# Reflecting q and k per head, one product for two, and raw gathers that take turns, in a graph attention kernel

## The chip, the cores and the metric

The kernel runs on one core of one Trainium2 chip. A core has five engines that run their own instruction streams: TensorE (PE, matrix products), VectorE (DVE), ScalarE (ACT), GpSimd (POOL) and SyncE (SP, which only issues transfers). They meet through semaphores. Matrix products land in a small memory called PSUM and everything else is worked on in SBUF; tensors in device memory are reached by DMA. The metric is the device time of the whole program in microseconds (us), as the median of several runs. Each run is compared with runs of the kernel before.

## The reference

One graph attention layer with a norm ahead of it. There are N = 12500 nodes with F = 128 features and E = 212500 edges, sorted by their destination `dst`. Each edge has 128 features of its own (`edge_h`) and a weight (`distance`).

```python
h = jnp.maximum(_layernorm(x, axis=-1), 0.0)          # node_h
q = (node_h @ Wq.T + bq).reshape(N, 8, 16)
k = (edge_h @ Wk.T + bk).reshape(-1, 8, 16)
v = (node_h @ Wv.T + bv).reshape(N, 8, 16)
qs, qd = q[src], q[dst]
in_m   = jnp.sum(qs * k,  axis=-1)
out_m  = jnp.sum(qd * k,  axis=-1)
diag_m = jnp.sum(qs * qd, axis=-1)
score = (softmax(in_m * SCALE) + softmax(out_m * SCALE)
         + softmax(diag_m * SCALE)) * distance ** lam   # softmax over the edges of each dst
h = segment_sum(score[..., None] * v[dst], dst)
return x + leaky_relu(h @ Wo.T + bo, 0.1)
```

The three sums are inner products within a head of 16 numbers. An orthogonal map of each head that is applied to q and to k leaves all three unchanged.

## The kernel before, in words

The edges are worked off in blocks of 512, each as 4 tiles of 128 edges (JN = 4). There are 415 full blocks, counted by `g`, and 20 edges left over ("few"). Five blocks (S = 5) make a tile `t`, one from each of five strands of the sorted edges; there are 83 tiles, and `s` is the strand of a block.

The order of the work is written out by hand: the helper `pin` chains every instruction that it is given to the one pinned before on the same engine, so that each engine runs in the order of the program text.

*Stage one* (the loop over `g` from -2 to 24) makes `q` of all nodes and stores it in a table in device memory, `q_table`. Each of its 25 turns takes 4 tiles of 128 nodes: statistics for the norm on DVE (L1064), the norm and rectifier on ACT (L932), a transpose on PE with a copy on ACT (L939, L941), q by PE from `wq` (L947), the bias added by DVE (L950), and the store by SP (L951). The list `side` puts other work between. The q rows of sources are later fetched by an indirect DMA of POOL (L706), 4 to a block, in the function `gather`. The first 24 blocks (RAW) are gathered from the raw `x`, before `q_table` exists, and normalized and projected later, in the loop; that is 96 gathers. 60 of these are issued at turn -2 and 36 at turn 9. Gathers from `q_table` begin after every turn has stored its part.

*The main loop* runs over the 415 blocks. For block `g` it issues, in this order: the gather of block g + 26 (LOOK = 26), the load of edge features, `turn(g + 2)` (PE transposes of the edge features, L1247, ACT copy L1249), `spread_q(g + 1)` (PE spreads q of the destinations over the edges by a one-hot matrix, L1264, ACT copy L1267), `project(g + 1)` (k by PE: a bias product L1254 over 512 columns, then four products with `wk`, L1256), `logits(g)` and `one_hots(g + 3)` (ACT, L697 and L698). `logits` is four DVE operations: source q by spread q (L1275), source q by k (L1276), spread q by k (L1277), and a reduction over the 16 numbers of a head of all three (L1278). After this come, depending on `s`, the segment softmax and the sums over destinations of an earlier tile (`turn_max`, `powers`, `show_ends` with L1423 to L1427, `to_rows` with L1437), and the node tiles that become due.

The table `behind` ties the four gathers of a block to PE's progress: the first (j = 0) of block g + 1 + 26 waits for PE's `turn`, the second for `spread_q`, the third for `project` and the fourth for the last PE instruction of the iteration. PSUM holds one buffer of `eT_ps` and two each of `k_ps` and `qd_ps`.

On PE the middle of the loop reads so, for one block of it (names: `eT_ps` the transposed edge features, `qd_ps` the spread q, `k_ps` the projected k, `oh` the one-hot matrix, `win` the q rows of the destinations):

```order
L1247 MATMUL eT_ps<-ident,ea 128x128 x4
L1264 LDWEIGHTS oh
L1264 MATMUL qd_ps<-win,oh 128x128
L1264 LDWEIGHTS oh
L1264 MATMUL qd_ps<-win,oh 128x128
L1264 LDWEIGHTS oh
L1264 MATMUL qd_ps<-win,oh 128x128
L1264 LDWEIGHTS oh
L1264 MATMUL qd_ps<-win,oh 128x128
L1254 LDWEIGHTS ones_88
L1254 MATMUL k_ps<-b_94,ones_88 128x512
L1256 MATMUL k_ps<-wk,eT 128x128 x4
```

The spread of q stands ahead of the projection, and the bias product, 512 columns wide, opens the projection.

Of the kernel before, what the change touches and what calls it, by code (L numbers as in the profile page):

```python
# [7 lines left out]
F32 = mybir.dt.float32  # L8
# [3 lines left out]
ALU = mybir.AluOpType  # L12
# [460 lines left out]
def ordered_path(ctx: ExitStack, tc: tile.TileContext, flag, x, src, dst, edge_attr, edge_weight,  # L473
# [102 lines left out]

    eps = consts.tile([P, 1], F32, name="eps")
# [17 lines left out]
    bv3, bk3, bo3 = [b3[:, i, None, :].to_broadcast([3, JN, F]) for i in range(3)]  # L595
    bq_all = consts.tile([P, F], F32, name="bq_all")
# [105 lines left out]
    def gather(g):  # L702
        if g < end:
            qq = qqs[g] = firsts[g] if g < FIRST else gath.tile([P, JN, F], F32, name="qq")
            for j in range(JN):
                rows = pin(nc.gpsimd.indirect_dma_start(  # L706
                    out=qq[:, j, :], out_offset=None, in_=x if g < RAW else q_table,
                    in_offset=bass.IndirectOffsetOnAxis(
                        ap=sources[g // S][:, g % S, j:j + 1], axis=0)))
# [63 lines left out]
    with tc.tile_pool(name="prep", bufs=1) as prep, \  # L773
# [4 lines left out]
        lam_sb = prep.tile([RW, 1], F32, name="lam_sb")  # L778
        w_in = prep.tile([P, 4, F], F32, name="w_in")
# [24 lines left out]
        pin(nc.sync.dma_start(bq_all, bq[None, :].to_broadcast([P, F])))  # L804
# [99 lines left out]

        def turn_w(i, to):
# [143 lines left out]
        turn_w(0, wq)  # L1049
# [189 lines left out]
    with tc.tile_pool(name="work", bufs=2) as work, \  # L1239
            tc.tile_pool(name="scan", bufs=2) as scan, \  # L1240
            tc.tile_pool(name="ps", bufs=1, space=PSUM) as ps:
        ks, eTs, qds, q_ps, lTs = {}, {}, {}, {}, {}
# [9 lines left out]
        def project(g):  # L1252
            k_ps = ks[g] = ps.tile([P, JN, F], F32, name="k_ps", bufs=2)
            pin(nc.tensor.matmul(k_ps, ones3, bk3, start=True, stop=False))  # L1254
            for j in range(JN):
                pin(nc.tensor.matmul(k_ps[:, j, :], eTs[g][:, j, :], wk, start=False,  # L1256
                                     stop=(j == JN - 1)))
            del eTs[g]

        def spread_q(g):  # L1260
            s, d = g % S, st[g // S]
            qd_ps = q_ps[g] = ps.tile([P, JN, F], F32, name="qd_ps", bufs=2)
            for j in range(JN):
                pin(nc.tensor.matmul(qd_ps[:, j, :], ohs[g][:, j * P:(j + 1) * P],  # L1264
                                     d["win"][:, s, :], start=(j == 0), stop=(j == JN - 1)))
            qds[g] = work.tile([P, JN, F], F32, name="qd")
            pin(nc.scalar.copy(qds[g], qd_ps))  # L1267
            del ohs[g]

        def logits(g):  # L1270
            s, t = g % S, g // S
            if s == 0:
                lTs[t] = scan.tile([P, JN, S, H3], F32, name="lT", bufs=4)
            prod = work.tile([P, JN, 3, F], F32, name="prod", bufs=1)
            pin(nc.vector.tensor_mul(prod[:, :, 1, :], qqs[g], q_ps[g]))  # L1275
            pin(nc.vector.tensor_mul(prod[:, :, 0, :], qqs[g], ks[g]))  # L1276
            pin(nc.vector.tensor_mul(prod[:, :, 2, :], qds[g], ks[g]))  # L1277
            pin(nc.vector.tensor_reduce(lTs[t][:, :, s, :],  # L1278
                                        prod.rearrange("p j i (h d) -> p j (i h) d", d=DIM), AX.X,
                                        ALU.add))  # L1280
            del ks[g], qds[g], q_ps[g], qqs[g]
# [397 lines left out]
        turn(0)  # L1679
        spread_q(0)  # L1680
        project(0)
        turn(1)
        raw_rectify(SOON)
        for g in range(end):
# [115 lines left out]
        names = ("eT_ps", "k_ps", "qd_ps", "qd_ps", "k_ps")  # L1800
        for r in range(len(rest) + 2):
            if r < len(rest):
# [5 lines left out]
                of.project_o(ps.tile([P, JN, F], F32, name=names[r], bufs=1 if r == 0 else 2))  # L1808
# [48 lines left out]
```

## Time and profile before

| what | value |
|---|---|
| median of 3 runs | 2730.74 us (2729.23 to 2732.47) |
| profiled execution | 2727.95 us |
| its span, first to last instruction | 2726.2 us |
| granted clock of PE, mean | 0.745 |
| busy share PE / DVE / ACT / POOL | 71% / 76% / 52% / 58% |
| stage one ends, first gather from `q_table` | 206.72 us |
| last gather | 2542.90 us |

In the profile each line of a group gives the source line, engine, operation, what it writes and reads, the count, then busy time in us and the mean of one in ns, then the idle time of the engine just ahead of it and what ended that. "remote" as the end of a wait is an event of a semaphore for which the profile shows no instruction; "issue" is time in which the engine waited for nothing that is shown. A timeline row gives start and length in us first.

### The profile page before, as it was taken

What the parts mean: (1) busy time and instruction counts of PE and PEld (TensorE: products, weight loads), DVE (VectorE), ACT (ScalarE), POOL (GpSimd) and SP (SyncE); (2) the same over time, 40 slices, a digit from 0 to 9 for tenths busy, and PEclk for the clock granted to TensorE, in tenths of its full rate; (3) what the DMA queues carried; (4) which work ended last, traced back from release to release, by engine and by line L of the source; (5) the groups of instructions that cost most, each with busy time, mean ns of one, the idle gap of its engine ahead of it and who ended that gap; (6) DMA issues with size and microseconds to landing.
All of it is one profiled execution on the core that took longest, in us unless ns stands there. A gap on an engine that the chain in (4) does not pass through costs nothing.

```text
span 2726.2 us, 37924 instructions
## 1 busy us (share of the span) xinstructions
PE 1941.1 (71%) x10956; PEld 1524.3 (56%) x10956; DVE 2071.3 (76%) x2887; ACT 1409.7 (52%) x2662; POOL 1585.3 (58%) x1683
## 2 busy tenths in 40 slices
PE   2366776777767777677777777777777776777885
PEld 1245655555555555555555655656556565555664
DVE  2265887777778778778877878877878787787995
ACT  1355864445555555555545555554545555555673
POOL 7516566666666666666666666666666666666200
PEclk9876887776777777777667767766767677776786
DMA  6256444544454454544445444444444544454431
GB/s 177 76 165 175 133 123 126 141 140 127 132 146 132 134 147 140 138 138 125 140 121 137 131 128 132 131 130 123 128 141 112 140 135 121 128 139 129 125 85 52
DMA packets 378950, 355.75 MB, mean 130 GB/s; under 512 B 192898, under 2 KB 298637, under 8 KB 378527
## 3 DMA queue, kind: packets, MB, share of 16 engines
q1 hardware_dynamic: 310109, 238.12, 30.6%
q0 software_dynamic: 53184, 108.92, 15.1%
q10 hardware_dynamic: 15440, 6.20, 0.9%
q8 instruction: 90, 1.47, 0.2%
q14 instruction: 127, 1.04, 0.1%
HBM read 320.83 MB, written 32.17 MB: 129 GB/s over the span
## 4 chain that ended last, share of the span: by engine, by line
PE 44%; DVE 16%; ACT 13%; another core or an unknown queue 12%; issue 11%; DMA 1%; DVEq 1%; POOL 1%; SPq 0%; ACTq 0%; POOLq 0%
PE k_ps L1256 12%; PE w_ps L1437 7%; PE eT_ps L1247 7%; DVE lT L1278 4%; PE qd_ps L1264 4%; PE k_ps L1254 3%; PE node_ps L1186 2%; DVE prod L1276 2%; ACT qd L1267 2%; ACT relb L697 2%; DVE prod L1275 2%; DVE prod L1277 2%; ACT oh L698 2%; PE m_ps L1381 2%
## 5 line engine op out<-in xcount | busy, mean ns | idle before, releaser
L706 POOL DMA_INDIRECT qq<-q_table,sources x1564 | 1479.2, 946 | 912.7 <-issue 336.7
L1278 DVE TENSOR_REDUCE lT<-prod 128x96 f32<-128x1536 f32 x415 | 727.4, 1753 | 14.3
L1256 PE MATMUL k_ps<-wk,eT 128*128 128x128 f32 x3320 | 621.5, 343 | 18.8 <-issue 17.1
L1256 PEld LDWEIGHTS k_ps<-wk,eT 128*128 128x128 f32 x3320 | 524.3, 240 | 171.6 <-issue 170.6
L1247 PE MATMUL eT_ps<-ident,ea 128*128 128x128 f32 x1660 | 346.5, 345 | 206.6 <-issue 129.7
L1276 DVE TENSOR_TENSOR prod<-qq,k_ps 128x512 f32<-128x512 f32 x412 | 280.7, 681 | 203.5 <-remote 166.3
L1247 PEld LDWEIGHTS eT_ps<-ident,ea 128*128 128x128 f32 x1660 | 247.9, 178 | 286.2 <-issue 173.1
L1249 ACT COPY eT<-eT_ps 128x512 f32<-128x512 f32 x415 | 240.7, 580 | 322.8 <-remote 122.6
L1267 ACT COPY qd<-qd_ps 128x512 f32<-128x512 f32 x415 | 244.8, 590 | 313.1 <-PE qd_ps L1264 88.5
L1437 PE MATMUL w_ps<-back,sel 128*126 128x144 f32 (+1 forms) x1296 | 232.1, 356 | 169.0 <-ACT sel L1427 134.4
L1275 DVE TENSOR_TENSOR prod<-qq,qd_ps 128x512 f32<-128x512 f32 x412 | 279.9, 679 | 89.2 <-issue 47.9
L1437 PEld LDWEIGHTS w_ps<-back,sel 128*126 128x126 f32 (+1 forms) x1296 | 218.2, 247 | 183.4 <-ACT sel L1427 144.2
L697 ACT ACTIVATE relb<-relb,before 126x512 bf16<-126x512 bf16 x415 | 303.1, 730 | 0.0
L1277 DVE TENSOR_TENSOR prod<-qd,k_ps 128x512 f32<-128x512 f32 x415 | 281.8, 679 | 0.0
L698 ACT ACTIVATE oh<-relb 126x512 bf16<-126x512 bf16 x415 | 261.3, 630 | 13.2
L1264 PE MATMUL qd_ps<-win,oh 126*128 126x128 bf16 x1660 | 205.6, 258 | 26.6 <-issue 13.7
L1254 PE MATMUL k_ps<-b,ones 3*128 3x512 bf16 x415 | 191.4, 461 | 23.0 <-DVE prod L1277 10.9
L1264 PEld LDWEIGHTS <-oh 126*128 126x128 bf16 x1660 | 164.2, 120 | 48.0 <-issue 34.1
L1381 PE MATMUL m_ps<-ident,m 120*128 120x120 f32 x332 | 76.1, 364 | 107.6 <-issue 59.0
L1426 ACT ACTIVATE sel<-d_ps 128x420 f32<-128x420 f32 x168 | 78.5, 514 | 139.0 <-remote 127.7
L1391 ACT ACTIVATE back<-back 128x480 f32<-128x480 f32 x83 | 50.0, 602 | 142.6 <-DVE back L1390 63.2
L1381 PEld LDWEIGHTS m_ps<-ident,m 120*128 120x128 f32 x332 | 53.1, 215 | 124.5 <-issue 82.6
(234 smaller groups left out, 1934.9 us busy)
## 6 DMA issues: line engine op xcount, KB each, us to landing
ea<-in_edge_attr_dram SPq DMA_DIRECT2D x415, 256.0 KB
relb<-rel_d SPq DMA_DIRECT2D x83, 630.0 KB
qq<-q_table,sources POOLq DMA_INDIRECT x1564
win<-q_table SPq DMA_DIRECT2D x415, 31.5 KB
far<-far_d SPq DMA_DIRECT2D x84, 120.2 KB
q_table<-q SPq DMA_DIRECT2D x24, 384.0 KB
sums<-rows SPq DMA_DIRECT2D x411, 7.9 KB
q_table<-xq SPq DMA_DIRECT2D x24, 256.0 KB
```

Source lines behind the costliest of these rows:

```text
L697: pin(nc.scalar.activation(d, d, AF.Abs, bias=before[:K3]))
L698: pin(nc.scalar.activation(oh, d, AF.Relu, bias=1.0, scale=-1.0))
L706: rows = pin(nc.gpsimd.indirect_dma_start(out=qq[:, j, :], out_offset=None, in_=x if g < RAW else q_table, in_offset=bass.IndirectOffsetOn ...
L1247: pin(nc.tensor.transpose(eT_ps[:, j, :], eas[g][:, j * F:(j + 1) * F], ident))
L1256: pin(nc.tensor.matmul(k_ps[:, j, :], eTs[g][:, j, :], wk, start=False, stop=(j == JN - 1)))
L1264: pin(nc.tensor.matmul(qd_ps[:, j, :], ohs[g][:, j * P:(j + 1) * P], d["win"][:, s, :], start=(j == 0), stop=(j == JN - 1)))
L1267: pin(nc.scalar.copy(qds[g], qd_ps))
L1275: pin(nc.vector.tensor_mul(prod[:, :, 1, :], qqs[g], q_ps[g]))
L1276: pin(nc.vector.tensor_mul(prod[:, :, 0, :], qqs[g], ks[g]))
L1277: pin(nc.vector.tensor_mul(prod[:, :, 2, :], qds[g], ks[g]))
L1278: pin(nc.vector.tensor_reduce(lTs[t][:, :, s, :], prod.rearrange("p j i (h d) -> p j (i h) d", d=DIM), AX.X, ALU.add))
L1437: pin(nc.tensor.matmul(w_ps[:(hi - lo) * W, lo:hi].rearrange("p s c -> p (s c)"), d["sel"][:n, j, lo:hi, :].rearrange("p s w -> p (s w)"), ...
```

## The change

Three parts.

First, q and k are reflected per head. From the bias of k a reflection (Householder) is made for each head that maps this bias to a multiple of the first axis. It is applied to `wq` and `wk` when they are turned (a product with the reflected identity, `axes`, instead of a transpose) and to q's bias. The bias of k then has one number other than zero per head, and its product covers 4 x 8 = 32 columns; it comes after the four products with `wk`. The reflection is computed in `bring_to_size` before stage one's loop and `reflect` at its turn -2; `wq` is turned at turn -1, where before it was turned ahead of the loop.

Second, k and the spread q of a block lie in one PSUM tile `qk_ps`, with two buffers, and one DVE product of 1024 elements multiplies both by the source q. `project` comes ahead of `spread_q`, and the second gather of a block waits for `project`, the third for `spread_q`.

Third, in stage one the raw gathers of blocks 0 to 5 are issued at turn -2 and those of each later block at turn (5 x block - 30) // 4, so four gathers at a time, the first of which waits for the last PE instruction pinned in that turn.

```diff
+    turned = consts.tile([P, 2, F], F32, name="turned")
+    axes, bq_all = turned[:, 0], turned[:, 1]
+    bk_all = consts.tile([P, F], F32, name="bk_all")
+    pin(nc.scalar.dma_start(bk_all, bk[None, :].to_broadcast([P, F])))
+    pin(nc.scalar.dma_start(bq_all, bq[None, :].to_broadcast([P, F])))
...
+    bk_lead = b3[:, 1, None, 0::DIM].to_broadcast([3, JN, HEADS])
...
-                if (g - LOOK, j) in behind:
-                    tc.add_manual_dep(rows.ins, behind[g - LOOK, j], mybir.DependencyInfo(
+                held = behind.get((g - LOOK, j), held)
+                if held is not None:
+                    tc.add_manual_dep(rows.ins, held, mybir.DependencyInfo(
                         mybir.DependencyClass.Sync, mybir.DependencyReason.SCHED_ONLY),
                         reason="close behind the products")
+                held = None
...
-            for i, b in enumerate((bv, bk, bo)):
+            for i, b in ((0, bv), (2, bo)):
                 pin(nc.sync.dma_start(b_row[:, i, :], b[None, :]))
+            pin(nc.vector.memset(b_row[:, 1, :], 0.0))
+            pin(nc.vector.tensor_copy(b_row[:, 1, 0::DIM], mirror["lead"][0:1]))
...
+        def bring_to_size():
+            small = room[:, 3 * F:3 * F + 8 * HEADS].rearrange("p (i h) -> p i h", h=HEADS)
+            top, low, size, square, side, lead, half, scale = [small[:, i] for i in range(8)]
+            pin(nc.vector.tensor_reduce(top, heads_of(bk_all), AX.X, ALU.max))
+            pin(nc.vector.tensor_reduce(low, heads_of(bk_all), AX.X, ALU.min))
...
+            pin(nc.vector.reciprocal(top, size))
+            v, w = room[:, :F], room[:, F:3 * F].rearrange("p (i f) -> p i f", i=2)
+            pin(nc.vector.tensor_mul(heads_of(v), heads_of(bk_all),
+                                     top[:, :, None].to_broadcast([P, HEADS, DIM])))
+            pin(nc.vector.tensor_mul(w[:, 0], v, v))
+            pin(nc.vector.tensor_reduce(square, heads_of(w[:, 0]), AX.X, ALU.add))
+            pin(nc.scalar.activation(low, square, AF.Sqrt))
...
+        def reflect():
...
+            pin(nc.vector.tensor_copy(axes, ident))
+            v_both = v[:, None, :].to_broadcast([P, 2, F])
+            pin(nc.vector.tensor_mul(w, turned, v_both))
+            along = room[:, 3 * F + 8 * HEADS:3 * F + 10 * HEADS]
+            pin(nc.vector.tensor_reduce(along, w.rearrange("p i (h d) -> p (i h) d", d=DIM), AX.X, ALU.add))
...
+            pin(nc.vector.tensor_sub(turned, turned, w))
...
-            pin(nc.tensor.transpose(w_ps, w_in[:, i, :], ident))
+            if i in (0, 2):
+                pin(nc.tensor.matmul(w_ps, w_in[:, i, :], axes, start=True, stop=True))
+            else:
+                pin(nc.tensor.transpose(w_ps, w_in[:, i, :], ident))
...
-        turn_w(0, wq)
+        bring_to_size()
...
+            if g == -2:
+                reflect()
             if 0 <= g + 1 < GN:
                 turn_h(g + 1)
+            if g == -1:
+                turn_w(0, wq)
...
-            if g == -2:
-                for of in range(3 * S):
-                    gather(of)
+            for of in range(RAW):
+                turn = (5 * of - 30) // 4
+                if max(turn, -2) == g:
+                    gather(of, pinned[str(mybir.EngineType.PE)] if g >= 0 else None)
             aside(g)
             if g == 9:
                 fetch_few()
-                for of in range(3 * S, RAW):
-                    gather(of)
...
         def project(g):
-            k_ps = ks[g] = ps.tile([P, JN, F], F32, name="k_ps", bufs=2)
-            pin(nc.tensor.matmul(k_ps, ones3, bk3, start=True, stop=False))
+            qks[g] = ps.tile([P, 2, JN, F], F32, name="qk_ps", bufs=2)
+            k_ps = qks[g][:, 0]
             for j in range(JN):
-                pin(nc.tensor.matmul(k_ps[:, j, :], eTs[g][:, j, :], wk, start=False,
-                                     stop=(j == JN - 1)))
+                pin(nc.tensor.matmul(k_ps[:, j, :], eTs[g][:, j, :], wk, start=(j == 0), stop=False))
+            pin(nc.tensor.matmul(k_ps.rearrange("p j (h d) -> p j h d", d=DIM)[:, :, :, 0], ones3, bk_lead,
+                                 start=False, stop=True))
...
-            qd_ps = q_ps[g] = ps.tile([P, JN, F], F32, name="qd_ps", bufs=2)
+            qd_ps = qks[g][:, 1]
...
-            pin(nc.vector.tensor_mul(prod[:, :, 1, :], qqs[g], q_ps[g]))
-            pin(nc.vector.tensor_mul(prod[:, :, 0, :], qqs[g], ks[g]))
-            pin(nc.vector.tensor_mul(prod[:, :, 2, :], qds[g], ks[g]))
+            pin(nc.vector.tensor_mul(prod[:, :, 0:2, :].rearrange("p j i f -> p i j f"),
+                                     qqs[g][:, None].to_broadcast([P, 2, JN, F]), qks[g]))
+            pin(nc.vector.tensor_mul(prod[:, :, 2, :], qds[g], qks[g][:, 0]))
...
             if g + 1 < end:
+                project(g + 1)
+                behind[g + 1, 1] = pinned[products]
                 spread_q(g + 1)
-                behind[g + 1, 1] = pinned[products]
-                project(g + 1)
                 behind[g + 1, 2] = pinned[products]
```

On PE the same block of the main loop now reads so (`qk_ps` holds k in its first half and the spread q in its second):

```order
L1308 MATMUL eT_ps<-ident,ea 128x128 x4
L1317 MATMUL qk_ps<-wk,eT 128x128 x4
L1318 LDWEIGHTS ones_92
L1318 MATMUL qk_ps<-b_98,ones_92 128x32
L1326 LDWEIGHTS oh
L1326 MATMUL qk_ps<-win,oh 128x128
L1326 LDWEIGHTS oh
L1326 MATMUL qk_ps<-win,oh 128x128
L1326 LDWEIGHTS oh
L1326 MATMUL qk_ps<-win,oh 128x128
L1326 LDWEIGHTS oh
L1326 MATMUL qk_ps<-win,oh 128x128
```

The projection has moved ahead of the spread, and the bias product is the projection's last and 32 columns wide.

On POOL, in stage one, the gathers of raw rows around the 24th read so before, with the semaphores that each waits for (DMASW and DMAHW are transfers, PE is TensorE's):

```order
L706 DMA qq<-in_x_dram,sources 128x128 [waits DMAHW3_49,DMASW4_49]
L706 DMA qq<-in_x_dram,sources 128x128 [waits DMASW5_49]
L706 DMA qq<-in_x_dram,sources 128x128 [waits DMASW6_49]
L706 DMA qq<-in_x_dram,sources 128x128 [waits DMASW7_49]
L706 DMA qq<-in_x_dram,sources 128x128 [waits DMASW0_49]
L706 DMA qq<-in_x_dram,sources 128x128 [waits DMASW1_49]
```

and so in the changed kernel:

```order
L711 DMA qq<-in_x_dram,sources 128x128 [waits DMAHW4_49,DMASW4_49]
L711 DMA qq<-in_x_dram,sources 128x128 [waits DMASW5_49]
L711 DMA qq<-in_x_dram,sources 128x128 [waits DMASW6_49]
L711 DMA qq<-in_x_dram,sources 128x128 [waits DMASW7_49]
L711 DMA qq<-in_x_dram,sources 128x128 [waits DMASW0_49,PE_49]
L711 DMA qq<-in_x_dram,sources 128x128 [waits DMASW1_49]
```

The fifth row, the first gather of a block, now waits for PE as well.

More of the change, by code (lines that the diff above doesn't have):

```diff
@@ L594, in ordered_path @@
     b3 = consts.tile([3, 3, F], BF, name="b3")
-    bv3, bk3, bo3 = [b3[:, i, None, :].to_broadcast([3, JN, F]) for i in range(3)]
-    bq_all = consts.tile([P, F], F32, name="bq_all")
+    bv3, bo3 = [b3[:, i, None, :].to_broadcast([3, JN, F]) for i in (0, 2)]
+    bk_lead = b3[:, 1, None, 0::DIM].to_broadcast([3, JN, HEADS])
     inv = consts.tile([P, NI], F32, name="inv")
@@ L700, in ordered_path, with gather @@
     raw = {k: consts.tile([P, RAW, JN], F32, name=f"raw_{k}") for k in ("inv", "shift")}
-    def gather(g):
+    def gather(g, held=None):
         if g < end:
@@ L778, in ordered_path @@
         lam_sb = prep.tile([RW, 1], F32, name="lam_sb")
+        room = node.tile([P, JN * 3 * F // 2], F32, name="room", tag="q3", bufs=2)
         w_in = prep.tile([P, 4, F], F32, name="w_in")
@@ L1799, in ordered_path @@
             halves_of(ab, engine)
-        names = ("eT_ps", "k_ps", "qd_ps", "qd_ps", "k_ps")
+        places_o = [ps.tile([P, JN, F], F32, name="eT_ps", bufs=1)]
+        for r in range(2):
+            qk_ps = ps.tile([P, 2, JN, F], F32, name="qk_ps", bufs=2)
+            places_o += [qk_ps[:, 0], qk_ps[:, 1]]
         for r in range(len(rest) + 2):
@@ L1807, in ordered_path @@
                 of.turn(small([P, JN, P], "node_ps"))
[L1808 removed]
+                of.project_o(places_o[r])
             if 0 <= r - 2:
```

28 lines of the change are left out of this document (24 added, 4 removed).

## The prediction

> **What bounds the kernel now.** I began with the page: its head, the busy shares, the slices and the costliest groups.
>
> ```profile
> span 2726.2 us, 37924 instructions
> PE 1941.1 (71%) x10956; PEld 1524.3 (56%) x10956; DVE 2071.3 (76%) x2887; ACT 1409.7 (52%) x2662; POOL 1585.3 (58%) x1683
> POOL 7516566666666666666666666666666666666200
> L706 POOL DMA_INDIRECT qq<-q_table,sources x1564 | 1479.2, 946 | 912.7 <-issue 336.7
> L1278 DVE TENSOR_REDUCE lT<-prod 128x96 f32<-128x1536 f32 x415 | 727.4, 1753 | 14.3
> L1276 DVE TENSOR_TENSOR prod<-qq,k_ps 128x512 f32<-128x512 f32 x412 | 280.7, 681 | 203.5 <-remote 166.3
> L1275 DVE TENSOR_TENSOR prod<-qq,qd_ps 128x512 f32<-128x512 f32 x412 | 279.9, 679 | 89.2 <-issue 47.9
> L1264 PE MATMUL qd_ps<-win,oh 126*128 126x128 bf16 x1660 | 205.6, 258 | 26.6 <-issue 13.7
> L1254 PE MATMUL k_ps<-b,ones 3*128 3x512 bf16 x415 | 191.4, 461 | 23.0 <-DVE prod L1277 10.9
> L1437 PE MATMUL w_ps<-back,sel 128*126 128x144 f32 (+1 forms) x1296 | 232.1, 356 | 169.0 <-ACT sel L1427 134.4
> ```
>
> No engine is full: DVE is busy 76% of the span, PE 71%, POOL 58%. The shares therefore do not name the bound, and the stages have to be looked at apart. The next view gives busy time by stretch (start and end in us, length, busy time and instruction count of PE, weight loads, DVE, ACT, POOL, then granted clock, DMA share, GB/s); below it the same for the reduce of each block (L1278) alone, whose count is the number of blocks finished.
>
> ```profile
> 20.00:115.00 95.00, 12.57 (x41) 8.66 (x41) 7.11 (x31) 8.10 (x19) 63.91 (x68) 0.92 0.37 100
> 150.00:200.00 50.00, 40.71 (x203) 30.00 (x203) 36.66 (x128) 36.18 (x90) 0.00 (x0) 0.83 0.60 178
> 300.00:2450.00 2150.00, 1583.39 (x8896) 1245.85 (x8895) 1699.66 (x2155) 1126.20 (x2073) 1364.55 (x1443) 0.73 0.48 132
> 2550.00:2660.00 110.00, 90.12 (x614) 72.73 (x612) 107.53 (x138) 77.77 (x153) 1.67 (x4) 0.86 0.34 97
> ```
> ```profile
> 300.00:2450.00 2150.00, 632.25 (x361) 0.73 0.48 132
> 2550.00:2660.00 110.00, 40.31 (x23) 0.86 0.34 97
> ```
>
> The main loop makes 361 blocks in 2150 us, 5.96 us each. At the end, where no gathers are left, it makes 23 in 110 us, 4.78 each, with DVE busy 107.53 of 110. So DVE bounds a block only where POOL has nothing to do. Where POOL gathers, a block needs four gathers. How far apart they are, and what holds them, is in POOL's part of the waits (total us, times, longest) and in a stretch of the timeline.
>
> ```profile
> POOL qq L706 <- issue: 310.6, 1004, 2.1
> POOL qq L706 <- remote: 213.5, 137, 2.5
> POOL qq L706 <- PE qd_ps L1264: 79.2, 66, 2.2
> POOL qq L706 <- PE k_ps L1256: 46.3, 47, 3.0
> DVE prod L1276 <- remote: 162.4, 78, 3.6
> ```
> ```profile
> 1295.77 0.88 PE L1423 MATMUL d_ps<-shows,ends_t 21*128 21x420 bf16 x2
> ...
> 1298.73 2.04 PE L1256 MATMUL k_ps<-wk,eT 128*128 128x128 f32 x8
> 1299.65 0.94 POOL L706 DMA_INDIRECT qq<-q_table,sources  x1 [0.30 <-issue]
> ...
> 1300.90 0.94 POOL L706 DMA_INDIRECT qq<-q_table,sources  x1 [0.30 <-issue]
> ...
> 1303.57 0.69 DVE L1276 TENSOR_TENSOR prod<-qq,k_ps 128x512 f32<-128x512 f32 x1 [3.26 <-remote]
> 1303.60 0.93 ACT L1426 ACTIVATE sel<-d_ps 128x420 f32<-128x420 f32 x2 [5.16 <-remote]
> 1303.80 0.94 POOL L706 DMA_INDIRECT qq<-q_table,sources  x1 [1.95 <-remote]
> ```
>
> Two gathers in a row start 1.25 us apart (1299.65, 1300.90), so four take 5.00 us of a block's 5.96; the other 0.96 is pauses. The stretch shows what a pause is. PE's matmul L1423 ends at 1296.65, and ACT, which reads its result, starts at 1303.60; PE's projection of k ends at 1300.77, and DVE starts on it at 1303.57; POOL, gated on PE too, starts at 1303.80. Three engines that wait for different PE results go within 0.23 us of each other, just after POOL has stood for 1.95 us. I read this so: while POOL issues gathers back to back, word of PE's finished work reaches the other engines late, and a pause of POOL lets it through. The waits agree: 137 pauses put down to "remote", 213.5/137 = 1.56 us each, and 113 more to the two PE lines on whose work gathers are gated. The loop is thus paced by POOL's gathers and by how often POOL has to stop for a PE signal, and not by how long PE or DVE work.
>
> Stage one, before the loop, has the same trouble in a worse form.
>
> ```profile
> DVE xq L950 <- remote: 90.0, 4, 31.4
> ACT hT L941 <- remote: 63.5, 3, 30.8
> ```
> ```profile
> 20.00:115.00 95.00, 6.23 (x24) 5.35 (x24) 0.92 0.37 100
> 150.00:200.00 50.00, 17.46 (x96) 15.29 (x96) 0.83 0.60 178
> ```
> ```profile
> L706 POOL DMA_INDIRECT ends_ab<-in_x_dram,sources x12: 940/944/1109, 4.6 to 18.5; - x12
> 206.72 0.94 POOL L706 DMA_INDIRECT qq<-q_table,sources  x1 [59.62 <-DMA qq<-in_edge_attr_dram]
> ```
>
> The fence with two stretches is the q matmul of stage one (L947), eight per turn: 3 turns in 95 us while 60 gathers of raw rows run back to back, 12 turns in 50 us (4.2 us each) while POOL is idle. DVE waits up to 31.4 us for a PE result there. The first gather from the finished table starts at 206.72.
>
> **The change part by part.** The profiled execution took 2727.95 us, 2.8 below the median of the runs shown (2730.74, 2729.23 to 2732.47); I sum against it. What can be told from no change is 0.2%, 5.5 us.
>
> *Reflection of q and k.* It adds 22 small DVE operations, one square root on ACT and two loads on ACT's queue, and takes one load off SP's; turning wq moves behind them. The nearest rows are the tiny operations and the 128-wide statistics of stage one.
>
> ```profile
> L1064 DVE BATCH_NORM_STATS2 stats<-xq 128x6 f32<-128x128 f32 x82 | 17.3, 278 | 0.9 <-DMA xq<-in_x_dram 0.8
> L758 DVE TENSOR_TENSOR sums<-stats 128x8 f32<-128x8 f32 (+5 forms) x8 | 1.5, 182 | 0.3
> ```
>
> Eleven work on 8 or 16 numbers a row (11 x 0.182 = 2.0 us), eleven on 128 or 256 (11 x 0.278 = 3.1): 5.1 us ahead of the first q. All of it counts if DVE's order holds the first turn, nothing if that turn waits behind the gathers anyway: 0 to +6 with the root. I take +3. The load of the biases' row loses one SP transfer and gains two DVE operations, 0.4 us beside a stretch in which DVE is busy 7.11 of 95: nothing; without that cover +0.4.
>
> *Raw gathers taking turns.* Instead of 60 in a row and later 36, 24 run at the start and then four per turn in 18 of the 25 turns, the first of each four held until PE has ended that turn. The number of gathers is unchanged. 24 gathers from 4.6 on, 1.25 apart, end at 34.6, and word of PE comes some 3 us later (the 1303.60 above is 2.70 after the gather at 1300.90): 38. A turn with four gathers is four times 1.25 and one pause of 1.56: 6.56 us; 18 of them 118. Seven turns without gathers at 4.2: 29. Sum 185, against 206.72: -22. Bounds: if the turns hide the gathers, 38 + 25 x 4.2 = 143, so -64; if each turn runs only after its gathers, 38 + 18 x (5.0 + 4.2) + 29 = 233, so +26. I take the middle one, since the loop overlaps gathers and PE work the same way. The cover of the turn is POOL's pause; if a turn needs two passes of PE to ACT and back, it needs a second pause, 18 x 1.56 = +28. Behind the held gather stand only later gathers; they are read by projections in the loop.
>
> *Bias of k in 32 columns, and order of PE.* 415 matmuls of 512 columns (461 ns) become 32-column ones. None as narrow is in the trace; the spread of q with 128 columns costs 205.6/1660 = 0.124 us each, and less than that leaves 0.03. I take 0.06: 0.40 us a block, 361 x 0.40 = 144 us of PE work in the long stretch. It is PE time beside POOL's pace, where PE is busy 1583.39 of 2150 already: bounds 0 and -144. I take -10, for the pauses in which POOL waits on a k matmul that has not ended; those are few, because the stretch above shows the pause 3.0 us after the matmul ended. The weight count on PE stays one bias, four k, four spread.
>
> *One product for k and q of destinations.* Two DVE operations of 512 elements (679 + 681 = 1360 ns) become one of 1024. The line through 512 at 0.680 and the reduce's 1536 at 1.753 gives 0.680 + 512 x 0.00105 = 1.217 us: 0.143 saved a block. Hidden where POOL paces (bounds 0 and -361 x 0.143 = -52), counted in full for the last 26 blocks, where DVE is full: 26 x 0.143 = -4. I take -5 in the loop. The price: the one product waits for both results, the old one over the spread (L1275) ran while k was still under way. Per block that is at most 0.68 us, on the 78 occasions where DVE waited for k: +53 at the worst, if DVE were the bound at these places; since POOL's pause ends the wait there, I take 0. The copy of q to SBUF by ACT (L1267) now comes after the last matmul, beside the longer product, which covers it; without that cover it costs 0.59 us a time.
>
> *Sum.* +3 - 22 - 10 - 5 - 4 = -38: 2727.95 - 38 = 2690. Its own range: stage one between -45 and 0, loop between -40 and 0: 2645 to 2720.
>
> **Rivals.**
>
> A. The engines' work decides after all. Then shorter PE and DVE work counts: 144 + 52 us in the long stretch, 4 in the last blocks and 19 in stage one and front, 2728 - 219 = 2509 at the most, and about 2600 when half of the 196 counts. For it: DVE at 76% and PE at 71%. Against: at the end, without gathers, the same work with the same PE takes 4.78 us a block, and DVE is 98% busy there. This mechanism has a page behind it: the Trainium skill, "Perfetto Trace Analysis", section "Tensor Engine Instruction (MATMUL, LD_WEIGHTS)", says that the end of a matmul in a profile is an estimate and that the semaphore update waits until the results are acknowledged. By that rule the late release could be array work not yet done, and PE's saving would be worth all of it: 2728 - 219 = 2509. The trace speaks against it by its quiet stretches: 12 turns in 50 us with no POOL instruction, with the same matmuls.
>
> B. Slower: the order of spread and k costs POOL pauses. The second gather of a block is now held by the longer k projection, and the one product by the last of three PE groups. If one more gather per five-block tile finds its signal not yet come, that is 83 pauses of 1.56 us, +129, so 2690 + 129 = 2820; if one in three tiles, +43, 2733. It is slower than now from 38/1.56 = 24 more pauses on. For it: 137 + 113 pauses already come from PE signals, and DVE waits 162.4 us for k. Against: the number of PE groups a block is unchanged, and k's group is shorter by 0.40 us.
>
> C. The held gathers of stage one gain nothing, because each turn still waits for word of PE (an outcome inside its bounds of -64 and +26). Then the reflection's +3 and the loop's -19 are left: 2728 + 3 - 19 = 2712. For it: the rows of L950 and L941, 31 us at a time behind gathers; four gathers in a turn are still 5 us of silence.
>
> **How the numbers follow.** Forecast 0.42, A 0.15, B 0.27, C 0.16. The time predicted is that of the forecast, 2690. Faster by over 0.2%: the forecast but for its last part (0.40), A (0.15), C for the most (0.12), together 0.67; slower: B, 0.27; the rest, 0.06, is the same. The range goes to A's 2600 below and to 2760 above, which leaves out A's lower part (0.06) and B's larger one (0.13).
>
> **What would show it.** Right: the first gather from the table near 185 us, no wait of 20 us at L950's successor in stage one; the merged product near 1.22 us, the bias below 0.12; about 361 reduces in 2150 us or up to six more; about as many POOL waits for "remote" and for the two PE lines as the 250 now; the last blocks at 4.64 us. Wrong: the table's first gather at 206 or later (C); 380 and more reduces in the stretch (A); over 300 such POOL waits and fewer reduces (B). A stall of DVE at the merged product that ends without a pause of POOL would mean that the reading of the late signals is wrong.

## The result and the profile after

The changed kernel takes 2683.71 us (median of 5 runs, 2679.88 to 2688.19) against 2729.23 us (2725.88 to 2732.47): a ratio of 0.983, 95% interval 0.9816 to 0.9844, or 45.5 us less. The forecast was 2690, a gain of 38 against the profiled execution.

One thing has to be known to understand the numbers further down. In the experiments the same kernel before took 2730.76 us on the chip of one group of runs and about 2175 us on the chips of the four other groups, in every run there. I call them the first kind of chip (the prediction and the result are of this kind) and the second kind; whether it is the chip or a lasting state of it, no run here tells. A time is judged only beside the kernel before on the same chip.

The page of the changed kernel, in the rows that answer to those shown of before:

```profile
span 2681.9 us, 37518 instructions
PE 1799.5 (67%) x10958; PEld 1484.4 (55%) x10958; DVE 2048.9 (76%) x2496; ACT 1400.6 (52%) x2663; POOL 1589.3 (59%) x1683
DVE  4648887777777777777778777777777787777995
L711 POOL DMA_INDIRECT qq<-q_table,sources x1564 | 1482.0, 948 | 858.2 <-issue 363.6
L1337 DVE TENSOR_TENSOR prod<-qq,qk_ps 128x1024 f32<-128x1024 f32 x412 | 501.4, 1217 | 341.9 <-ACT qd L1329 169.2
```

One more group row gives the narrow bias, from the view by lines:

```profile
L1318 PE MATMUL qk_ps<-b,ones 3*128 3x32 bf16 x415 | 91.4, 220 | 2.4 <-issue 2.4
```

PE is busy 141.6 us less and DVE 22.4 us less, and, as the stretches show, none of it shortened the loop. Busy time by stretch (columns as in the prediction), and the reduce of each block alone:

```profile
20.00:115.00 95.00, 51.65 (x211) 35.99 (x212) 49.63 (x186) 42.96 (x100) 63.34 (x65) 0.73 0.54 149
300.00:2450.00 2150.00, 1455.39 (x8850) 1206.69 (x8848) 1669.79 (x1777) 1100.10 (x2037) 1368.55 (x1445) 0.75 0.48 132
```
```profile
300.00:2450.00 2150.00, 632.84 (x361) 0.75 0.48 132
```

In the loop's 2150 us PE works 128.0 us less than before (1583.39 to 1455.39) and DVE 29.9 us less (1699.66 to 1669.79), and 361 blocks are finished, as before. In the first stretch it is the other way round: where PE was busy 12.57 us of 95 it now is 51.65. The timeline of POOL dates it:

```profile
8.33 1.11 POOL L711 DMA_INDIRECT ends_ab<-in_x_dram,sources  x1 [4.96 <-DMA sources<-in_src_dram]
...
149.07 0.95 POOL L711 DMA_INDIRECT qq<-in_x_dram,sources  x1 [0.31 <-issue]
157.56 0.95 POOL L711 DMA_INDIRECT qq<-q_table,sources  x1 [7.54 <-DMA qq<-in_edge_attr_dram]
```
```profile
2494.10 0.95 POOL L711 DMA_INDIRECT qq<-q_table,sources  x1 [0.30 <-issue]
```
```profile
2617.55 1.75 DVE L1340 TENSOR_REDUCE lT<-prod 128x96 f32<-128x1536 f32 x1
```

The same three moments of the kernel before:

```profile
206.72 0.94 POOL L706 DMA_INDIRECT qq<-q_table,sources  x1 [59.62 <-DMA qq<-in_edge_attr_dram]
```
```profile
2542.90 0.94 POOL L706 DMA_INDIRECT qq<-q_table,sources  x1 [0.30 <-issue]
```
```profile
2665.33 1.75 DVE L1278 TENSOR_REDUCE lT<-prod 128x96 f32<-128x1536 f32 x1
```

| stretch | before | after | difference |
|---|---|---|---|
| start to first gather from the table | 206.72 | 157.56 | -49.2 |
| first to last gather from the table | 2336.18 | 2336.54 | +0.4 |
| last gather to last reduce | 122.4 | 123.5 | +1.0 |
| last reduce to the end | 60.9 | 64.4 | +3.5 |
| span | 2726.2 | 2681.9 | -44.3 |

So, by the traces, the whole gain is stage one's, and the loop gained nothing. POOL's waits in the loop (the stretch from 300 to 2450 us) after and, for two of the names, before:

```profile
POOL qq L711 <- remote: 104.7, 73, 2.6
POOL qq L711 <- PE eT_ps L1308: 83.2, 60, 2.2
POOL qq L711 <- PE qk_ps L1326: 70.2, 48, 2.2
POOL qq L711 <- PE m_ps L1443: 48.2, 29, 3.2
```
```profile
POOL qq L706 <- PE eT_ps L1247: 27.0, 22, 1.9
POOL qq L706 <- PE m_ps L1381: 15.4, 12, 3.3
```
```profile
DVE prod L1337 <- ACT qd L1329: 162.7, 74, 5.9
```

The waits put down to "remote" fell from 213.5 to 104.7 us, while those put down to PE's transposes rose from 27.0 to 83.2 and those to m_ps from 15.4 to 48.2. The names changed, the total did not: POOL is idle 785.4 of the 2150 us before (2150 less 1364.55 busy) and 781.4 after. DVE's longest item of waiting ahead of a product has another name too, and the same length (162.7 us in 74 times; 162.4 in 78 before).

### The profile page after: what moved, and what is told of

Same layout as the page of the kernel before. It is cut to its first block, busy times and chain, and to the rows that moved or that the text cites. A ratio compares the mean times of both kernels' runs of the same rounds, so it can differ in the third digit from the quotient of the medians.

```text
span 2681.9 us, 37518 instructions
## 1 busy us (share of the span) xinstructions
PE 1799.5 (67%) x10958; PEld 1484.4 (55%) x10958; DVE 2048.9 (76%) x2496; ACT 1400.6 (52%) x2663; POOL 1589.3 (59%) x1683
## 4 chain that ended last, share of the span: by engine, by line
PE 43%; ACT 15%; DVE 15%; issue 14%; another core or an unknown queue 9%; DMA 1%; DVEq 1%; POOL 1%; SPq 0%; ACTq 0%; POOLq 0%
PE qk_ps L1317 12%; PE eT_ps L1308 9%; PE w_ps L1499 5%; PE qk_ps L1326 4%; DVE prod L1337 4%; DVE lT L1340 4%; ACT qd L1329 3%; ACT relb L702 3%; ACT eT L1310 2%; PE m_ps L1443 2%; DVE prod L1339 2%; PE node_ps L1247 2%; PE d_ps L1485 2%; PE qk_ps L1318 2%
## 5 line engine op out<-in xcount | busy, mean ns | idle before, releaser
L711 POOL DMA_INDIRECT qq<-q_table,sources x1564 | 1482.0, 948 | 858.2 <-issue 363.6
L1337 DVE TENSOR_TENSOR prod<-qq,qk_ps 128x1024 f32<-128x1024 f32 x412 | 501.4, 1217 | 341.9 <-ACT qd L1329 169.2
L1317 PE MATMUL qk_ps<-wk,eT 128*128 128x128 f32 x3320 | 597.1, 338 | 72.0 <-issue 30.5
L1317 PEld LDWEIGHTS qk_ps<-wk,eT 128*128 128x128 f32 x3320 | 555.3, 252 | 85.5 <-DVE prod L1339 34.7
L1329 ACT COPY qd<-qk_ps 128x512 f32<-128x512 f32 x415 | 244.3, 589 | 676.3 <-PE qk_ps L1326 177.3
L1339 DVE TENSOR_TENSOR prod<-qd,qk_ps 128x512 f32<-128x512 f32 x415 | 282.0, 680 | 0.0
L1326 PE MATMUL qk_ps<-win,oh 126*128 126x128 bf16 x1660 | 197.0, 250 | 8.4 <-issue 8.2
L1400 DVE TENSOR_TENSOR_SCAN l_ps<-far,carry,l_ps 120x512 f32<-120x512 bf16 x80 | 102.5, 1282 | 22.1 <-remote 11.6
L711 POOL DMA_INDIRECT qq<-in_x_dram,sources x84 | 82.0, 976 | 44.8 <-issue 23.5
L1431 DVE TENSOR_TENSOR_SCAN m<-far,head,l_ps 120x512 f32<-120x512 bf16 x81 | 102.9, 1271 | 0.0
L1452 DVE TENSOR_TENSOR back<-lT,m_ps 128x480 f32<-128x480 f32 x83 | 53.9, 649 | 61.5 <-PE qk_ps L1318 17.2
```

Source lines behind the costliest of these rows:

```text
L711: rows = pin(nc.gpsimd.indirect_dma_start(out=qq[:, j, :], out_offset=None, in_=x if g < RAW else q_table, in_offset=bass.IndirectOffsetOn ...
L1337: pin(nc.vector.tensor_mul(prod[:, :, 0:2, :].rearrange("p j i f -> p i j f"), qqs[g][:, None].to_broadcast([P, 2, JN, F]), qks[g]))
L1339: pin(nc.vector.tensor_mul(prod[:, :, 2, :], qds[g], qks[g][:, 0]))
```

## The experiments

Theory P, from the prediction: on this chip the loop is paced by POOL's gathers and by how late PE's word comes while they are issued, so that PE's and DVE's savings are hidden, and the gain comes from stage one. Rival E: the engines' work counts, and the loop stands still only because the later product eats what the narrow bias and the single product save. Rival L is its other half, that the single product loses by waiting for both results.

**Each part alone or undone.** `turns_only` is the kernel before with the third part only, `turns_undone` the changed kernel with stage one as before, `wide_bias` and `two_products` take back one saving of the loop each.

```diff
--- before, turns_only
-            if g == -2:
-                for of in range(3 * S):
-                    gather(of)
+            for of in range(RAW):
+                turn = (5 * of - 30) // 4
+                if max(turn, -2) == g:
+                    gather(of, pinned[str(mybir.EngineType.PE)] if g >= 0 else None)
...
-                for of in range(3 * S, RAW):
-                    gather(of)
--- after, turns_undone: the same lines the other way round
--- after, wide_bias
-    bk_lead = b3[:, 1, None, 0::DIM].to_broadcast([3, JN, HEADS])
+    bk_lead = b3[:, 1, None, :].to_broadcast([3, JN, F])
...
--- after, two_products
-            pin(nc.vector.tensor_mul(prod[:, :, 0:2, :].rearrange("p j i f -> p i j f"),
-                                     qqs[g][:, None].to_broadcast([P, 2, JN, F]), qks[g]))
+            pin(nc.vector.tensor_mul(prod[:, :, 0, :], qqs[g], qks[g][:, 0]))
+            pin(nc.vector.tensor_mul(prod[:, :, 1, :], qqs[g], qks[g][:, 1]))
```

> The kernel before with the third part alone: raw gathers four to a turn in stage one, the first of each held for PE. Theory P (POOL's gathers and the late word of PE pace the loop, so that all of the gain lies in stage one): the first gather from the table at about 155 us instead of 206.7, the loop unchanged at 361 blocks in 300 to 2450 us, time 2729 - 50 = 2679, between 2672 and 2687. Rival E (the engines' own work counts, and in the changed kernel its saving in the loop was lost again by the later product): this kernel has neither, so it also gives about 2680; this run tells only how much stage one is worth. Rival X (the turns gain only together with the shorter work of PE): above 2700.

> The changed kernel with the raw gathers of stage one as before (60 at the start, 36 at turn 9), reflection, narrow bias and one product kept. Theory P: 2729 + 3 for the reflection and the same end, between 2722 and 2738. Rival E, if the saved work counted in the loop: below 2700.

> The changed kernel with the bias product of k again over all 512 columns (zeros in 480 of them, the result the same): it adds 0.461 - 0.220 = 0.24 us of PE to each block, 100 us over 415. Theory P: hidden, 2680 to 2692. Rival E: at least half of it counts, 2734 to 2784.

> The changed kernel with two products of 512 elements instead of one of 1024, order of PE kept: adds 0.143 us of DVE to a block, 59 us over 415. Theory P: hidden in the loop, 4 us in the last 26 blocks: 2680 to 2694. Rival E: at least half counts, 2713 to 2743. Rival L (the one product loses by waiting for both results what it saves; k's product alone can start while the spread is under way): 2670 or less.

These ran on a chip of the second kind, where the kernel before took 2175.51 us. No expectation in absolute time could hold there.

| kernel | us | ratio to before, 95% interval |
|---|---|---|
| turns_only | 2175.28 | 1.0002 (0.9993 to 1.0011) |
| turns_undone | 2168.88 | 0.9965 (0.9952 to 0.9979) |
| wide_bias | 2169.97 | 0.9972 (0.9961 to 0.9983) |
| two_products | 2180.87 | 1.0027 (1.0016 to 1.0038) |

On this chip the turns of stage one, alone, are worth nothing, where the table of stretches puts the whole gain into stage one on the first kind. The changed kernel itself has no run on the second kind, so the other parts can only be read from its variants: the bias's width seems to be worth about 1 us (wide_bias beside turns_undone), and one product instead of two about 11 us (two_products beside wide_bias). To see why, the changed kernel and a test of POOL's pace went next. `fourth_plain` takes one POOL gather of four out of each block from block 29 on, with the wait of that gather for PE, and loads 128 consecutive rows of the table by SP in its place, so that a quarter of the edges lack their own source rows.

```diff
             for j in range(JN):
+                if j == 3 and g >= AHEAD:
+                    pin(nc.sync.dma_start(qq[:, j, :], q_table[g * 24:g * 24 + P, :]))
+                    continue
                 rows = pin(nc.gpsimd.indirect_dma_start(
```

> The changed kernel itself once more, beside the kernel before on the same chip. On the chip of the four runs ahead of this one the kernel before took 2175.5 us and not 2729, DVE was busy 98% of the loop and no gather of the loop waited for PE by more than 0.8 us. If the chip is of that kind: theory D (there DVE sets the pace, and the gain is what the one product saves of DVE's time, less 3 us for the reflection): 2165 to 2172, ratio about 0.997; theory P as first stated, that POOL paces the loop everywhere and stage one's 49 us come off the end: 2126. If the chip is of the first kind, 2729 before: 2684 again.

> The changed kernel with the fourth gather of each block (from block 29 on) replaced by a plain load of 128 consecutive rows of the table on SP's queue, so that a quarter of the edges get the wrong source rows: the bytes and the work of PE, DVE and ACT stay, POOL issues three gathers a block instead of four. On a chip with 2729 us before: theory P (POOL's gathers pace the loop and delay word of PE): a block goes from 5.96 to about 4.8 us, where DVE is full, 2684 - 360 x 1.1 = 2290, between 2200 and 2400; rival E (engines' own work): 2670 to 2700. On a chip with 2175 before: DVE is the bound, so no change against the changed kernel, within 10 us.

This chip was of the first kind (before: 2730.76 us). The changed kernel took 2679.94 us, ratio 0.9814 (0.9798 to 0.9831), as at first. `fourth_plain` took 2217.95 us, ratio 0.8119 (0.8106 to 0.8132): 462 us less than the changed kernel, with one of POOL's four gathers gone from a block while PE, DVE and ACT did the same work. Theory P had given 2200 to 2400, rival E 2670 to 2700. Its loop stretch and its reduces:

```profile
300.00:2000.00 1700.00, 1310.50 (x8806) 1084.97 (x8804) 1646.37 (x1778) 1086.40 (x2027) 1026.70 (x1083) 0.81 0.60 167
```
```profile
300.00:2000.00 1700.00, 631.02 (x360) 0.81 0.60 167
```

A block takes 4.72 us, and DVE is busy 1646.37 of 1700, 97%. So on the first kind of chip POOL's gathers set the pace, and without a quarter of them DVE does. Three things went together in this run, though: the instruction of POOL, its scattered transfer, and one of the four waits for PE. Which of them gave how much is not separated.

**The same kernels again, for a chip of the first kind.** `gates_02` is the changed kernel with two of the four waits of a block's gathers taken out. `turns_only_b`, `wide_bias_b` and `two_products_b` repeat the kernels above, and `turns_only_c` repeats the first a third time.

```diff
-                held = behind.get((g - LOOK, j), held)
+                held = behind.get((g - LOOK, j), held) if j in (0, 2) else None
```

> The same kernel as turns_only (the kernel before with the third part alone), for a chip on which the kernel before takes 2730 us; there it can show what stage one is worth. Theory P there: all of the gain, 2680 plus or minus 8, the loop at 361 blocks in 2150 us. Rival C2 (the reflection, the narrow bias and the one product carry part of it): 2695 or more. On a chip with 2175 before: 2175 again.

> The same kernel as wide_bias (512 columns of bias again, 0.24 us of PE more per block, 100 us over 415), for a chip with 2730 us before. Theory P there: hidden, within 10 us of the changed kernel's 2680 to 2684. Rival E (PE's work counts, and in the changed kernel its saving was eaten by the later product): 2730 or more. On a chip with 2175 before: 2170 again.

> The same kernel as two_products (one product of 1024 split again in two of 512, order of PE kept), for a chip with 2730 us before. Theory P there: within 10 us of 2680. Rival L (the one product, which waits for both results, loses what it saves): below 2665. Rival E: above 2700. On a chip with 2175 before: 2181 again.

> The changed kernel with two of the four waits of a block's gathers on PE taken out (the second's and the fourth's; they set an order and guard no data). On a chip with 2730 before: if each wait costs a pause of its own when it comes, the 252 pauses of 1.69 us become about half, and the loop gains up to 200 us: 2480 to 2600; theory P with a need (PE's word passes only while POOL stands, so each block needs about as much pause whatever causes it): 2650 to 2720. On a chip with 2175 before: within 10 us of the changed kernel.

> The same kernel again (the kernel before with the third part alone). On a chip with 2730 us before: theory P, 2680 plus or minus 8 with the loop at 361 blocks in 300 to 2450 us; rival C2 (the other two parts carry part of the gain), 2695 or more. On a chip with 2175 before: 2175 a third time.

All five landed on chips of the second kind (before 2174.99 and 2175.07 us). They repeat the first group: turns_only_b 2174.82, ratio 1.0001 (0.9992 to 1.001); turns_only_c 2174.08, 0.9997 (0.9988 to 1.0006); wide_bias_b 2168.9, 0.9977 (0.9968 to 0.9985); two_products_b 2181.11, 1.0026 (1.0017 to 1.0036). `gates_02` gives 2168.38, 0.9971 (0.9963 to 0.998). With two waits fewer its time is that of turns_undone and wide_bias, so these two waits of the loop cost nothing there; what they cost on the first kind was not measured.

**What the second kind of chip shows.** A row of the page of `turns_only_c` (third group of runs, kernel before with the turns), and a stretch of its timeline:

```profile
L706 POOL DMA_INDIRECT qq<-q_table,sources x1564 | 1481.9, 948 | 477.7 <-issue 223.1
```
```profile
1000.27 0.60 PE L1248 MATMUL eT_ps<-ident,ea 128*128 128x128 f32 x4
...
1000.84 0.95 POOL L706 DMA_INDIRECT qq<-q_table,sources  x1 [0.30 <-issue]
1000.91 0.59 ACT L1250 COPY eT<-eT_ps 128x512 f32<-128x512 f32 x1 [0.46 <-PE eT_ps L1248]
...
1002.09 0.95 POOL L706 DMA_INDIRECT qq<-q_table,sources  x1 [0.30 <-issue]
```

POOL issues gathers back to back here too, 1.25 us apart, yet PE's transpose ends at 1000.87 and ACT starts on it at 1000.91. On the first kind ACT started 6.95 us after PE's end in the prediction's stretch (on another product, L1423). The gathers' idle time is 477.7 us over 1564, little more than the bare 0.30 us between two of them; on the first kind it is 912.7 before and 858.2 after. PE's work itself is about as long on both: the projection of k, by line,

```profile
L1257 PE MATMUL k_ps<-wk,eT 128*128 128x128 f32 x3320 | 596.8, 334 | 2.5 <-ACT eT L1250 2.5
```

334 ns here and 343 in the same product on the first kind. The rule that rival A of the prediction rested on, in the Trainium skill, "Perfetto Trace Analysis", section "Tensor Engine Instruction (MATMUL, LD_WEIGHTS)", that a profile's matmul ends are estimates and the semaphore comes only after the acknowledgement, does not by itself account for the 7 us: the wait after the estimated end can be as short as 0.04 us on the second kind, with matmuls of the same shapes. On the first kind itself `fourth_plain` does the same PE work in 4.72 us a block.

On the second kind two limits lie close together. POOL is hardly ever held: turns_only_c's last gather starts at 2090.8, and 1660 gathers at 1.25 us from 4.7 on would end at 2080. That holds in stage one too: the first gather from the table starts at 127.6 with the turns and at 131.1 without them (turns_undone), where it was 206.72 on the first kind before the change. So on these chips there was no gap in stage one for the turns to close.

```profile
L706 POOL DMA_INDIRECT qq<-q_table,sources x1564: 942/947/1309, 127.6 to 2090.8; - x196
```
```profile
L711 POOL DMA_INDIRECT qq<-q_table,sources x1564: 940/944/1432, 131.1 to 2095.4; - x196
```

DVE makes 360 blocks in 1700 us and is busy 98% of it:

```profile
300.00:2000.00 1700.00, 1398.68 (x8785) 1107.32 (x8784) 1667.80 (x2134) 1079.90 (x2025) 1285.83 (x1358) 0.80 0.60 164
```

```profile
300.00:2000.00 1700.00, 631.13 (x360) 0.80 0.60 164
```

1358 gathers in 1700 us are 339.5 blocks, 360 are used up: the lead of the gathers shrinks until both end together. A faster DVE therefore gains only until it has caught up with the gathers. From 2000 to 2120 us wide_bias_b's DVE, with the single product, waits for gathers that have not landed; in the same stretch of two_products_b and turns_only_c there is no such row:

```profile
DVE prod L1337 <- DMA qq<-q_table,sources: 6.7, 3, 2.5
```

**Both savings of the loop taken back together.** `wide_two` is wide_bias and two_products in one; it keeps the turns, the order of PE and the common tile.

> The changed kernel with both savings of the loop taken back: 512 columns of bias (0.24 us of PE more a block) and two products (0.053 us of DVE more a block, by the busy time of DVE with and without, 2048.8 and 2026.6 over 415 blocks). What stays is the turns of stage one, the order of PE and the common tile. On a chip with 2730 before: theory P, 2678 to 2692, since nothing in the loop is set by these two; rival E, the savings counted and were eaten by the later product: 2734 to 2800. On a chip with 2175 before: theory D, as two_products, 2178 to 2185, since PE's part is hidden by DVE.

It ran beside 2174.68 us and took 2186.25, ratio 1.0041 (1.0027 to 1.0055), on a chip of the second kind again. That is 5 us above two_products and 1 us above the interval that theory D allowed (D, from `after_again`: on the second kind DVE sets the pace). There a wider bias costs about 1 us while DVE's product is single (wide_bias against turns_undone) and about 5 by the medians when there are two, though the runs of wide_two (2179.41 to 2187.31) overlap those of two_products (2177.21 to 2185.02) and come from another chip. Out of some 100 us of PE work that is little: PE is hidden behind DVE, not quite completely. No test on the first kind separates the loop's parts.

## Why the prediction was right, and where its sum was not

*Bound by POOL and by late word of PE.* That POOL's gathers set the pace is right on the first kind of chip, and shown by `fourth_plain`: 462 us for one gather in four, its transfer and its wait included. The reading of the cause went too far, in two ways. The prediction has it that back-to-back gathers delay PE's word; on the second kind the same gathers at the same 1.25 us delay nothing that can be seen, so that gathers are not enough for it. Something of the chip or its state has to be added, and no run here shows what. And the prediction has it that a pause of POOL lets the word through; it named as a sign against this a stall of DVE at the merged product that ends without such a pause. There are such stalls: of the 131 waits of 1 us or more ahead of L1337 between 300 and 2450 us, 103 overlap a pause of POOL longer than 0.6 us and 28 do not. In one of the 28, PE's last spread ends at 475.87 by the profile, ACT's copy of it starts 1.82 us later between gathers that run back to back, and DVE follows:

```profile
475.26 0.61 PE L1326 MATMUL qk_ps<-win,oh 126*128 126x128 bf16 x4
475.69 0.94 POOL L711 DMA_INDIRECT qq<-q_table,sources  x1 [0.30 <-issue]
...
476.94 0.95 POOL L711 DMA_INDIRECT qq<-q_table,sources  x1 [0.30 <-issue]
477.69 0.59 ACT L1329 COPY qd<-qk_ps 128x512 f32<-128x512 f32 x1 [1.40 <-remote]
...
478.19 0.95 POOL L711 DMA_INDIRECT qq<-q_table,sources  x1 [0.30 <-issue]
...
478.31 1.22 DVE L1337 TENSOR_TENSOR prod<-qq,qk_ps 128x1024 f32<-128x1024 f32 x1 [1.89 <-issue]
```

So the word is late, but a pause is not needed for it to come. As POOL itself waits for PE, pauses and late words would also fall together if both only waited for the same thing.

*Stage one, -22.* The largest term, and mis-sized: it measured -49.2 with the reflection in it. The sum had put 18 turns with gathers and 7 without one after another, 118 and 29 us behind a start of 38. The last raw gather starts at 149.07 and the table's first gather 8.5 us after it, so that most of the seven turns without gathers lay beside gathers of other turns. And 18 pauses of 1.56 us, 28 us, were too many: between the first gather into `qq` and the last raw one, 83 steps of 1.25 us fill 104 of 125.5 us,

```profile
L711 POOL DMA_INDIRECT qq<-in_x_dram,sources x84: 941/947/2585, 23.6 to 149.1; - x84
```

which leaves 22, in about ten pauses and a few longer gathers. The bound of -64 was nearer than the middle value, but by another course than the one behind it: there the turns hide the gathers, and here the gathers run nearly without a gap and the turns lie behind them. The waits for PE in stage one became shorter as well, and none of 20 us is left. Up to the table's first gather they are

```profile
DVE xq L1008 <- remote: 26.5, 4, 16.0
```
```profile
ACT hT L999 <- remote: 20.2, 3, 12.0
```

against 95.2 and 71.1 us up to it before (the prediction's rows, 90.0 and 63.5, end at 120 us). That the held gathers cause this is read from the trace and not shown by a run: on the first kind the turns were run neither alone nor undone.

*Reflection, +3.* The start of POOL moved by 3.7 us, from 4.6 to 8.33, but by another cause than the one counted: the wait ahead of it names the load of the source indices (4.96 us), while the working counted DVE operations. The size fits by chance, and how much of it reached the end of stage one is not separated.

*Narrow bias, -10.* The PE time saved was over-rated: 220 ns for 32 columns and not 60, so that the saving is 0.24 us a block and not 0.40. The nearest row had been read as 0.124 us, the busy time of the spread divided by its count; its four products of a block overlap, and one of them lasts 258 ns. The narrow bias is worth nothing in the loop (361 blocks in 2150 us before and after) and, by wide_bias beside turns_undone, about 1 us on the second kind.

*One product, -5 and -4.* Its duration came out as worked out, 1217 ns. What it saves did not: DVE's operations start before the one ahead has ended (in two stretches of the second kind the two products take steps of 0.61 and 0.59 us, and the single one starts 1.11 us ahead of its successor), so a duration is longer than its step, and the steps save 0.09 us a block, not 0.143. DVE's busy time falls by 22.4 us, 0.054 us a block, with the operations of the reflection added to it; in the stretch from 300 to 2450 us, without them, it falls by 29.9 us over 361 blocks, 0.083. The loop kept its pace, since DVE waits 330 us ahead of the product instead of 282 before both:

```profile
L1337 DVE TENSOR_TENSOR prod<-qq,qk_ps 128x1024 f32<-128x1024 f32 x361 | 439.5, 1217 | 330.6 <-ACT qd L1329 162.7 <-issue 148.2 <-DMA qq<-q_table,sources 12.3
```
```profile
L1276 DVE TENSOR_TENSOR prod<-qq,k_ps 128x512 f32<-128x512 f32 x361 | 246.0, 681 | 196.7 <-remote 162.4 <-PE qd_ps L1264 8.3 <-PE m_ps L1381 7.0
L1275 DVE TENSOR_TENSOR prod<-qq,qd_ps 128x512 f32<-128x512 f32 x361 | 245.3, 679 | 85.8 <-issue 46.8 <-ACT qd L1267 34.0 <-DMA qq<-q_table,sources 2.0
```

The saved time of DVE became waiting, 48 us more of it. The last blocks, -4 by the same wrong step, took 1.0 us more, and the end after them 3.5 more, for which there was no term; where the 3.5 us come from stays open.

*The rivals.* A: the counts of its kind (380 blocks in the stretch) did not come. B: POOL's idle time in the loop did not grow (785.4 and 781.4 us), and nothing in the loop became slower. Whether the later product costs something on the first kind that the savings just cover is not excluded, since the kernels that could tell it only ran on the second kind; there two_products is slower than turns_only by 5.6 and 6.3 us. POOL's first gather starts 3.5 us later in it (8.2 against 4.7 us), which may be a part of this; the order of PE and the common tile are in it too. C: wrong, stage one gained.

So that the forecast of 2690 came near 2683.71 is luck in its size: two errors met. Stage one with the reflection gave 30 us more than the -22 and +3 counted for it, and loop and end gave 24 us less than the -19 counted for them. What was right in the mechanism is that POOL's gathers pace the loop, that no saving of PE and DVE shows in the loop's time, and that the gain is in stage one.

## What to carry to other kernels

Ask of each stage which engine it waits for, and follow a saving to that wait: 128 us less PE work and 30 us less DVE work in a stretch bought no block here, while stage one, where POOL's early gathers were spaced out, became 49 us shorter on the kind of chip where word of PE comes late. Count an operation by the distance of starts in a full stretch, not by its duration. And measure a gain on more than one chip: it is 45 us on the first kind, and the nearest variants of the changed kernel (turns_undone, wide_bias, gates_02) gained 5.5 to 6.6 us on the second, where the turns alone gained nothing.

## What the hardware showed that I had not expected

The same kernel takes 2730 us on some chips and 2175 on others, while gathers in a row are 1.25 us apart on both and the k product is 343 and 334 ns long. Most of the difference of some 555 us is waiting of POOL: 912.7 us of idle time ahead of its table gathers against 477.7 (turns_only_c, whose time on the second kind is that of the kernel before). A projection bias of 32 columns, one product by itself, took 220 ns, where one of 128 columns of the spread, in a group of four that overlap, took 250. What makes PE's word late on the first kind was not found.
